# Moving the source dot products of a graph-attention layer one layer later, into the loop that uses them

## The chip, the cores and the metric

The kernel runs on one core of a Trainium2 chip. The metric is device time in microseconds (us), from the start of the program on the core to its end. One core has five engines that run side by side, each with an instruction queue of its own: PE (TensorE, matrix products), DVE (VectorE), ACT (ScalarE), POOL (GpSimd) and SP (SyncE, which here only issues transfers). Transfers are carried out by DMA engines; SP, ACT and POOL each issue some.

## The reference

Four graph-attention layers follow each other on 4096 nodes with 256 features. All use the same 0/1 matrix `adj` (4096 x 4096), and each ends in a layer norm of `x` plus the layer's result. Cut to what the change touches, with the layers counted from one:

```
x1 = layernorm(x  + additive attention with 4 heads(x, adj))
x2 = layernorm(x1 + scaled dot-product attention with 4 heads(x1, adj))
# third layer: additive attention with one head
h     = x2 @ W
e_src = h @ a[:256, 0]
e_dst = h @ a[256:, 0]
e     = leaky_relu(e_src[:, None] + e_dst[None, :], 0.01)
att   = softmax(where(adj > 0, e, -1e12), axis=1)
x3 = layernorm(x2 + elu(att @ h))
out = layernorm(x3 + cosine attention(x3, adj))
```

In the third layer each row i of the result needs one number of its own, `e_src[i]`, and one for each neighbour, `e_dst[j]`. The kernel takes exponentials of both apart. With the part that cancels in the softmax left out, the weight of a pair is max(exp(0.99 e_src[i]) exp(e_dst[j]), exp(0.01 e_dst[j])), which is computed as relu(row * dst - own) + own.

## The kernel before

The features stay in SBUF in one tile `X`, as 32 tiles of 128 nodes. Every layer goes through 8 blocks of 512 result rows, and within a block through all 4096 neighbours: in the first layer by tiles of 128, in the second by 64 tiles of 64 (index j), in the third by 16 pairs of tiles (index g), in the fourth by 32 tiles. The order of the work on PE, DVE and ACT in the second and third layers is the order in which the Python code writes it (`manual_schedule`); in the fourth layer's loop only the ending is written out so, and a scheduler orders the rest. Work that belongs to a finished block is spread by hand over the steps of the next block: the `finish(b, j)` and `finish(b, g)` functions say which step does what. Three steps (`LAG = 3`) lie between making a pair's weights and multiplying with them.

The second layer (`multi_head_attention`) makes scores on PE (L810), exponentials on ACT (L812), multiplies with the mask on DVE (L822), sums the weights into a tile `den` for the row sums, in part on POOL (L832) and in part by accumulating transfers that POOL issues (L838, `den<-prob`), and multiplies with V on PE (L846). The eight `prob` buffers of DVE come free when PE and these transfers have read them. The `finish` of a block turns, scales and normalises its 512 rows of x2. Four of its steps then make the dot products for the third layer, one tile at a time: `ga.dots(t)` multiplies the tile with two vectors in `a_row` (n = 0 for the source, n = 1 for the destination) and adds up along the row (L502, into `dot`). Then `ga.factors(b)` at j=57 takes the exponentials: for the source `src` (L510), which L515 stores to DRAM in the order of the nodes (`far<-src`, 128 partitions x 4 values, 512 elements of four bytes, on ACT's queue), and for the destination `dst`, `own` and `less`, which stay in SBUF.

The last block of the second layer has no next block, so its finishing is a generator, `tail` (L855 joins the parts of `den`, L868 makes the row sums on PE, L876 and L883 transpose, the layer norm follows, and at the end come the dots and factors of block 7). The third layer's block 0 takes three steps of it in each pair from g=2 on.

The third layer (`additive_one`) needs for block b the 512 values of `src` as one row, the same in all 128 partitions. `ga.row(b)` (L521) reads it back from DRAM on SP's queue; it waits there until the store has landed. Odd blocks keep it in the tile `a_row`, which the dots no longer need by then, and even ones in `first_row`. In each pair `weights(b, g)` issues the mask (L549, SP's queue, four buffers), makes relu(row * dst - own) on ACT (L556), adds `own` and multiplies with the mask on DVE (L557), and, in all blocks but the first, mixes the weights for a multiplication with fewer products (L434 on DVE, L435 and L436 on POOL). PE multiplies with X (block 0, L571) or with the mixed parts (L444, seven products per pair). After pair 15 ACT and DVE take the sums out of the accumulators (L450 to L458, `quarters`), and PE goes on to reuse an accumulator when it has been read. `finish` projects the sums with W on PE (L586), takes the elu and normalises; beside it the fourth layer's inputs are prepared (`follow`, with transfers `far<-squares` and `xT<-far` on SP's queue).

The fourth layer (`cosine_attention`) starts with its own scores (L1105); at tile (0, 1) it calls the third layer's `tail`, which makes the projection of its last block (L586).

Of the kernel before, what the change touches and what calls it, by code (L numbers as in the profile page):

```python
# [9 lines left out]
FP = mybir.dt.float32  # L10
# [3 lines left out]
AF = mybir.ActivationFunctionType  # L14
# [4 lines left out]
P = 128  # L19
D = 256  # L20
KC = D // P
QB = 4
QW = QB * P
# [5 lines left out]
def kernel(  # L29
# [27 lines left out]
    nc = tc.nc  # L57
    N = x.shape[0]
    NT = N // P
    NB = N // QW  # L60

    def pool(stack, name, bufs, **kw):
        return stack.enter_context(tc.tile_pool(name=name, bufs=bufs, reuse_waits="tile", **kw))
# [3 lines left out]
    fin = ctx.enter_context(tc.tile_pool(name="fin", bufs=2))  # L67
# [397 lines left out]
    class Additive:  # L465
# [30 lines left out]
                nc.vector.scalar_tensor_tensor(w[:, c, :D], pm[:, :D], -1.0 / D, w[:, c, :D], OP.mult, OP.add)  # L496
                nc.vector.memset(w[:, c, D:D + 1], 1.0 / D)

        def dots(self, t):
            for n in range(2):  # L500
                junk = fin1.tile([P, QW], FP, name="kept0")[:, :D]
                nc.vector.tensor_tensor_reduce(junk, X[:, t, :D], self.a_row[:, n, :], 1.0, 0.0, OP.mult, OP.add,  # L502
                                               self.dot[:, t, n:n + 1])

        def factors(self, b):

            t = slice(b * QB, (b + 1) * QB)
            s, d = self.dot[:, t, 0], self.dot[:, t, 1]
            src = fin.tile([P, QB], FP, name="src2")
            nc.scalar.activation(src, s, AF.Exp, scale=1.0 - self.slope)  # L510
            nc.scalar.activation(self.dst[:, t], d, AF.Exp)
            nc.scalar.activation(self.own[:, t], d, AF.Exp, scale=self.slope)
            nc.vector.tensor_scalar_mul(self.less[:, t], self.own[:, t], -1.0)
            far = self.rows[b] = self.far.tile([QB, P], FP, name=f"far2_{b}")
            nc.scalar.dma_start(far.rearrange("k p -> p k"), src)  # L515

        def row_of(self, b):
            return self.a_row.rearrange("p n f -> p (n f)") if b % 2 else self.first_row

        def row(self, b, eng):  # L520
            eng.dma_start(self.row_of(b), self.rows[b].rearrange("k p -> (k p)").unsqueeze(0).to_broadcast([P, QW]))  # L521
# [1 line left out]
    def additive_one(w_sb, ga, tail, op, follow):  # L523

        with ExitStack() as lay:
            mp = pool(lay, "gb_mask", 4)
            zp = pool(lay, "gb_z", 4)
            keep = pool(lay, "gb_mixed", 1)
# [15 lines left out]
            def weights(b, g):  # L544
                if b == 0 and g < 2:
                    mask = ga.first_mask[:, 2 * g:2 * g + 2, :]
                else:
                    mask = mp.tile([P, 2, QW], I32, name="mask")
                    nc.sync.dma_start(mask, edges[:, 2 * g:2 * g + 2, b * QW:(b + 1) * QW])  # L549
                if g == 13 and b < NB - 1:  # L550
                    ga.row(b + 1, nc.sync)
                z = prob[b, g] = zp.tile([P, 2, QW], FP, name="prob")
                for n in range(2):
                    j = 2 * g + n
                    r = pr.tile([P, QW], FP, name="r")
                    nc.scalar.activation(r, ga.row_of(b), AF.Relu, bias=ga.less[:, j:j + 1], scale=ga.dst[:, j:j + 1])  # L556
                    nc.vector.scalar_tensor_tensor(z[:, n, :], r, ga.own[:, j:j + 1], mask[:, n, :], OP.add, OP.mult)  # L557
                if b:
                    s = mix[b, g] = zp.tile([P, 4, HW], FP, name="mix")
                    mix_weights(s, z, nc.gpsimd)  # L560
# [74 lines left out]
            LAG = 3  # L635
# [3 lines left out]
            with tc.manual_schedule(engines=fixed):  # L639
                for i in range(len(units) + LAG):  # L640
                    b, g = units[i - LAG] if i >= LAG else (-1, 0)
                    if g == NP - 1:
                        sums(b, g)
                    if i < len(units):
                        weights(*units[i])
                    if b >= 0:
                        if g < NP - 1:
                            sums(b, g)
                        if b:
                            finish(b - 1, g)  # L650
                        else:
                            for _ in range(3 if g > 1 else 0):
                                next(before, None)
                            if g == 9:
                                follow.start()
                            elif g == 12:
                                follow.centre(bank())
                            if g % 2:
                                t = mixed[g // 2] = keep.tile([P, 2, 4, P], FP, name=f"mixed{g // 2}")
                                mix_features(t, g // 2)  # L660
                        if b > 1 and g in (2, 4, 6, 8, 9, 10, 11, 12, 13, 14, 15):
                            follow.prepare(bank, b - 2, 1, ys[b - 2])
                        if b == NB - 1 and g > 3 and g % 2 == 0:
                            q = g // 2 - 2
                            nc.scalar.dma_start(X[:, q * QB:(q + 1) * QB, :D], far_y[q])
                        if b == NB - 1 and g in (3, 5, 7):
                            follow.load_mask(0, (g - 3) // 2, prob[b, g][:, 0, :1])
# [11 lines left out]
    def multi_head_attention(w_sb, b_sb, tail, rows_of_den, rows_done, narrow_edges, ga):  # L679
# [12 lines left out]
        with ExitStack() as lay:  # L692
# [215 lines left out]
            def finish(b, j):  # L908

                rows = [X[:, b * QB + k, :D] for k in range(QB)]  # L910
                if j in (7, 9):
                    join_sums(b, j // 2 - 2)
                elif j == 12:
                    row_sums(halves(), b)
                elif j == 15:
                    bank = halves()
                    pd = turned_row_sums(bank, b)
                    po = turned_half(bank, b, 0)
                    reciprocals(pd, b)
                    half(po, b, 0)  # L920
                elif j == 18:
                    half(turned_half(halves(), b, 2), b, 2)
                elif j in (21, 23, 25, 27):
                    k = (j - 21) // 2
                    if k == 0:
                        mvs[b] = fin.tile([P, QB, 2], FP, name="mv")
                    one_row(mvs[b], k, rows[k])
                elif j == 29:
                    roots[b] = begin_root(mvs[b])
                elif j == 31:  # L930

                    end_root(*roots[b], nc.gpsimd)
                    lift_mean(mvs[b], *roots[b][:2], nc.gpsimd)
                elif j in (35, 37, 39, 41):
                    k = (j - 35) // 2
                    scale_row(rows[k], mvs[b], roots[b][1], k)
                if j + LAG - 1 in relief:

                    nc.vector.tensor_tensor(*late.pop(), OP.add)
                    ga.dots(b * QB + relief.index(j + LAG - 1))  # L940
                elif j == 57:
                    ga.factors(b)
                elif j == 63 and b == 1:
                    ga.row(0, nc.sync)
                elif j == 33 and b == NB - 2:
                    nc.gpsimd.dma_start(ga.first_mask, adjT.rearrange("(t p) i -> p t i", p=P)[:, :QB, :QW])
# [21 lines left out]
        def tail(bank):  # L968

            b = NB - 1  # L970
            for n in (1, 2):
                join_sums(b, n)
                yield
            yield
            row_sums(bank, b)
            yield
            yield
            reciprocals(turned_row_sums(bank, b), b)
            yield
            for k in (0, 2):  # L980
                half(turned_half(bank, b, k), b, k)
                yield
            mv = fin.tile([P, QB, 2], FP, name="mv")
            for k in range(QB):
                one_row(mv, k, X[:, b * QB + k, :D])
                yield
            v, r, n = begin_root(mv)
            yield
            end_root(v, r, n, nc.gpsimd)
            lift_mean(mv, v, r, nc.gpsimd)  # L990
            yield
            for k in range(QB):
                scale_row(X[:, b * QB + k, :D], mv, r, k)
                ga.dots(b * QB + k)
                yield
            ga.factors(b)
            rows_done()
            yield
# [78 lines left out]
    def cosine_attention(co, tail):  # L1077
# [4 lines left out]
        with ExitStack() as lay:  # L1082
# [137 lines left out]
            for i in range(len(units) + LAG):  # L1220
                if i < len(units):
                    b, j = units[i]
                    scores(b, j)
                    if j % 2:
                        weights(b, j // 2)
                    if (b, j) == (0, 1):
                        tail(bank, cp)
                    if (b, j) in steps:
                        n, step = steps[b, j]
                        co.prepare(bank, n, step, X[:, n * QB:(n + 1) * QB, :])  # L1230
# [104 lines left out]
```

## Time and profile before

| what | time |
|---|---|
| median of three runs | 2845.0 us (2840.16 to 2847.42) |
| profiled execution | 2831.88 us, of which 2830.1 us is the span of the profile |
| PE busy | 2784.8 us, 98% of the span |
| DVE / ACT / POOL busy | 2276.0 / 1694.8 / 1048.9 us |
| first layer | 0 to about 735 us |
| second layer, its loop over blocks | about 815 to 1728 us |
| third layer, block 0 | about 1728 to 1794 us |
| third layer, blocks 1 to 7 | about 1794 to 2190 us |
| fourth layer | about 2190 to 2830 us |

The profile comes from one execution. Busy time is the time in which an engine was carrying out an instruction. "A <- B: total, times, longest" in the list of waits means that engine and instruction group A was idle, and that B was what it last waited for. L numbers are lines of the kernel before; in the changed kernel the lines of the third layer stand 8 to 10 lower down.

### The profile page before, as it was taken

How to read it: one execution, taken by the hardware profiler on the slowest of the kernel's cores; microseconds unless marked ns; L12 is line 12 of the kernel's file. 1: busy time of each engine (PE TensorE's matmuls, PEld its weight loads, DVE VectorE, ACT ScalarE, POOL GpSimd, SP SyncE). 2: the span in 40 equal slices, each digit the busy share in tenths (PEclk: the TensorE clock that was granted, in tenths of full speed). 3: DMA queues.
4: the chain of work that ended last, by engine and by line, in shares of the span. 5: the costliest groups of instructions: out<-in, count | busy, mean ns of one | idle time of the engine just before them, and what ended most of it. 6: DMA issues, size and time to landing. Idle time of an engine off the chain costs nothing. (4 is left out here: it accounts for less than half of the span.)

```text
span 2830.1 us, 50179 instructions
## 1 busy us (share of the span) xinstructions
PE 2784.8 (98%) x19505; PEld 1433.5 (51%) x19505; DVE 2276.0 (80%) x3034; ACT 1694.8 (60%) x2641; POOL 1048.9 (37%) x983
## 2 busy tenths in 40 slices
PE   9999999999999999999999998999999999999998
PEld 4333333333543333333333333788888777777776
DVE  8899999999667778887887787888777766666665
ACT  8899999999246656666665655465555422222222
POOL 0001001010049878779778783345445000000000
PEclk9999999999999999999999999999999999999999
DMA  7566767665349898989999897566657544344341
GB/s 211 105 137 141 141 136 143 132 137 103 92 99 193 181 187 180 185 177 194 190 185 180 181 185 176 156 203 210 191 184 230 111 61 66 60 63 64 60 57 33
DMA packets 243650, 404.59 MB, mean 143 GB/s; under 512 B 25185, under 2 KB 126033, under 8 KB 242514
## 3 DMA queue, kind: packets, MB, share of 16 engines
q0 software_dynamic: 104176, 182.74, 40.8%
q1 hardware_dynamic: 132720, 211.41, 24.1%
q10 hardware_dynamic: 6514, 7.23, 0.7%
q8 instruction: 153, 2.51, 0.3%
q14 instruction: 87, 0.71, 0.1%
HBM read 332.27 MB, written 35.73 MB: 130 GB/s over the span
## 5 line engine op out<-in xcount | busy, mean ns | idle before, releaser
L822 DVE TENSOR_TENSOR prob<-p,mask 128x1024 f32<-128x1024 f32 x512 | 616.4, 1221 | 173.8 <-ACT p L812 136.9
L812 ACT ACTIVATE p<-p,shift 128x1024 f32<-128x1024 f32 x512 | 555.7, 1088 | 332.2 <-PE p L810 331.6
L310 PE MATMUL acc<-prob,V 128*32 128x512 f32 x6144 | 664.0, 592 | 1.2 <-DVE prob L300 1.2
L297 ACT ACTIVATE prob<-row,dst 128x512 f32<-128x512 f32 x1020 | 635.0, 712 | 0.6
L300 DVE SCALAR_TENSOR_TENSOR prob<-prob,mask 128x2048 f32<-128x2048 f32 x256 | 580.3, 2285 | 25.8 <-ACT prob L297 25.2
L832 POOL TENSOR_TENSOR den<-den,prob 128x1024 f32<-128x1024 f32 x220 | 557.4, 2534 | 81.7 <-DVE prob L822 73.7
L810 PE MATMUL p<-qT,kT 64*64 64x512 f32 x4096 | 533.2, 592 | 12.3 <-DVE prob L822 12.3
L846 PE MATMUL acc<-prob,V 64*64 64x512 f32 x4096 | 531.4, 590 | 0.0
L310 PEld LDWEIGHTS acc<-prob,V 128*32 128x32 f32 x6144 | 197.3, 110 | 453.0 <-issue 431.3
L444 PE MATMUL acc<-mix,mixed 128*128 128x256 f32 x1440 | 389.4, 380 | 1.4 <-DVE quarters L458 1.2
L810 PEld LDWEIGHTS p<-qT,kT 64*64 64x64 f32 x4096 | 154.0, 133 | 293.0 <-issue 232.8
L846 PEld LDWEIGHTS acc<-prob,V 64*64 64x64 f32 x4096 | 158.6, 133 | 282.0 <-issue 279.4
L444 PEld LDWEIGHTS acc<-mix,mixed 128*128 128x128 f32 x1440 | 271.9, 190 | 41.7 <-PE acc L444 3.5
L1117 DVE TENSOR_TENSOR prob<-prob,mask 128x1024 f32<-128x1024 f32 x128 | 156.5, 1223 | 167.1 <-ACT prob L1109 167.0
L90 POOL COPY tick<-prob 128x1 f32<-128x1 f32 x35 | 38.5, 1100 | 641.7 <-DVE prob L300 640.8
L838 POOL DMA_DIRECT2D den<-prob x240 | 223.2, 930 | 94.5 <-DMA den<-prob 41.4
L444 PE MATMUL acc<-prob,X 128*128 128x256 f32 x960 | 249.9, 380 | 6.4 <-DVE quarters L450 6.4
L1036 POOL DMA_DIRECT2D mask<-in_adjT x64 | 47.8, 747 | 518.8 <-DVE prob L1117 432.4
L557 DVE SCALAR_TENSOR_TENSOR prob<-r,own,mask 128x512 f32<-128x512 f32 x252 | 177.1, 744 | 72.3 <-POOL mix L436 24.2
L444 PEld LDWEIGHTS acc<-prob,X 128*128 128x128 f32 x960 | 181.1, 190 | 89.7 <-issue 61.7
L1109 ACT ACTIVATE prob<-p 128x512 f32<-128x512 f32 x144 | 86.2, 598 | 220.6 <-PE p L1105 208.6
L1109 ACT ACTIVATE prob<-g 128x512 f32<-128x512 f32 x112 | 66.8, 596 | 194.0 <-PE g L1105 194.0
(219 smaller groups left out, 2808.7 us busy)
## 6 DMA issues: line engine op xcount, KB each, us to landing
mask<-in_adjT SPq DMA_DIRECT2D x254, 512.0 KB
den<-prob POOLq DMA_DIRECT2D x240, 512.0 KB, 5.4
mask<-edges SPq DMA_DIRECT2D x512, 64.0 KB
mask<-in_adjT POOLq DMA_DIRECT2D x64, 512.0 KB, 5.6
edges<-in_adj POOLq DMA_DIRECT2D x32, 512.0 KB, 9.7
far<-squares SPq DMA_DIRECT2D x16, 512.0 KB
den<-prob SPq DMA_DIRECT2D x16, 512.0 KB
row<-far SPq DMA_DIRECT2D x7, 1024.0 KB
```

Source lines behind the costliest of these rows:

```text
L297: nc.scalar.activation(z[:, h, :], r, AF.Relu, bias=-1.0, scale=dst[:, j, h:h + 1])
L300: nc.vector.scalar_tensor_tensor(z, z, 1.0, mask[m][:, j % MJ, :].unsqueeze(1).to_broadcast([P, H, QW]), OP.add, OP.mult)
L310: nc.tensor.matmul(acc[b][h * G:(h + 1) * G, n, :], part, prob[b, j][:, h, :], start=(j == 0), stop=(j == NT - 1))
L444: nc.tensor.matmul(acc[at][:, half * HW:(half + 1) * HW], w, a, start=(g == 0 and half == 0), stop=(g == NP - 1), skip_group_check=True)
L557: nc.vector.scalar_tensor_tensor(z[:, n, :], r, ga.own[:, j:j + 1], mask[:, n, :], OP.add, OP.mult)
L810: nc.tensor.matmul(p[c * d:(c + 1) * d, r, :], kT[half, c, at:at + d], qT[half, c, cols], start=True, stop=True)
L812: nc.scalar.activation(p, p, AF.Exp, bias=shift)
L822: nc.vector.tensor_tensor(z, p, mask[m][:, j % MJ, :].unsqueeze(1).to_broadcast([P, KC, QW]), OP.mult)
L832: nc.gpsimd.tensor_tensor(to, to, flat, OP.add)
L838: nc.gpsimd.dma_start(to, flat, accum_op=OP.add)
L846: nc.tensor.matmul(acc[b][c][r * d:(r + 1) * d, :], V[half, j, r * d:(r + 1) * d], prob[b, j][half, r, :], start=(j == 0), stop=(j == NH - 1))
L1117: nc.vector.tensor_tensor(z, z, co.mask[b, 2 * g // MJ][:, lo:lo + 2, :], OP.mult)
```

## The change

Three things are moved.

First, `dots` takes a list of which dot products to make, and the tile for the unused elementwise product. In the second layer, `finish` makes both for block 0 and only the destination's for blocks 1 to 6, and the `tail` of block 7 makes only the destination's. The source's dot products for block b+1 are made in the third layer's block b, one tile in each of the pairs g=4 to 7. `factors` is cut in two: `sources(b)` has the exponential and the store of `src`. It runs in the second layer for block 0 (at j=59 instead of 57), and for block b+1 in the third layer's block b at g=8. The row is read back at g=11 instead of g=13. Since `a_row` is now in use in the third layer, odd blocks keep their row in a new tile `other_row`.

Second, the third layer's block 0 takes the steps of the second layer's `tail` from g=4 on instead of g=2, and the fourth layer's `start` and `centre` move from g=9 and 12 to g=11 and 14.

Third, the fourth layer calls the third layer's `tail`, with its last projection, at tile (0, 3) instead of (0, 1).

```diff
-        def dots(self, t):
-            for n in range(2):
-                junk = fin1.tile([P, QW], FP, name="kept0")[:, :D]
+        def dots(self, t, which, sb=fin1, name="kept0"):
+            for n in which:
+                junk = sb.tile([P, QW if sb is fin1 else D], FP, name=name)[:, :D]
                 nc.vector.tensor_tensor_reduce(junk, X[:, t, :D], self.a_row[:, n, :], 1.0, 0.0, OP.mult, OP.add,
                                                self.dot[:, t, n:n + 1])
...
+        def sources(self, b):
+            src = fin.tile([P, QB], FP, name="src2")
+            nc.scalar.activation(src, self.dot[:, b * QB:(b + 1) * QB, 0], AF.Exp, scale=1.0 - self.slope)
             far = self.rows[b] = self.far.tile([QB, P], FP, name=f"far2_{b}")
             nc.scalar.dma_start(far.rearrange("k p -> p k"), src)
...
-                if g == 13 and b < NB - 1:
-                    ga.row(b + 1, nc.sync)
+                if b < NB - 1:
+                    if 4 <= g < 4 + QB:
+                        ga.dots((b + 1) * QB + g - 4, (0,), sb, "h")
+                    elif g == 8:
+                        ga.sources(b + 1)
+                    elif g == 11:
+                        ga.row(b + 1, nc.sync)
...
-                            for _ in range(3 if g > 1 else 0):
+                            for _ in range(3 if g > 3 else 0):
                                 next(before, None)
-                            if g == 9:
+                            if g == 11:
                                 follow.start()
-                            elif g == 12:
+                            elif g == 14:
                                 follow.centre(bank())
...
-                    ga.dots(b * QB + relief.index(j + LAG - 1))
+                    ga.dots(b * QB + relief.index(j + LAG - 1), (1,) if b else (0, 1))
                 elif j == 57:
                     ga.factors(b)
+                elif j == 59 and b == 0:
+                    ga.sources(b)
...
-                ga.dots(b * QB + k)
+                ga.dots(b * QB + k, (1,))
...
-                    if (b, j) == (0, 1):
+                    if (b, j) == (0, 3):
                         tail(bank, cp)
```

More of the change, by code (lines that the diff above doesn't have):

```diff
@@ L507, in factors @@
             t = slice(b * QB, (b + 1) * QB)
-            s, d = self.dot[:, t, 0], self.dot[:, t, 1]
-            src = fin.tile([P, QB], FP, name="src2")
-            nc.scalar.activation(src, s, AF.Exp, scale=1.0 - self.slope)
+            d = self.dot[:, t, 1]
             nc.scalar.activation(self.dst[:, t], d, AF.Exp)
@@ L517, in row_of @@
         def row_of(self, b):
-            return self.a_row.rearrange("p n f -> p (n f)") if b % 2 else self.first_row
+            return self.other_row if b % 2 else self.first_row
         def row(self, b, eng):
@@ L525, in additive_one @@
         with ExitStack() as lay:
+            ga.other_row = pool(lay, "gb_row", 1).tile([P, QW], FP, name="other_row")
             mp = pool(lay, "gb_mask", 4)
```

## The prediction

> **What bounds the kernel now.** I read the page's engine table first, then the waits of TensorE stage by stage, then what the engine named there was itself waiting for, and last the DMA throughput in those places.
>
> ```profile
> span 2830.1 us, 50179 instructions
> ...
> PE 2784.8 (98%) x19505; PEld 1433.5 (51%) x19505; DVE 2276.0 (80%) x3034; ACT 1694.8 (60%) x2641; POOL 1048.9 (37%) x983
> ```
>
> PE is the bound. The change neither adds nor removes a matmul, so all that it can win is PE's idle time, some 36 us without the last wait at the end, and it can lose by adding to it. TensorE's waits in the second layer's loop (815 to 1728 us), and then in the third layer up to the fourth's start (1728 to 2200 us); total, times, longest:
>
> ```profile
> PE p L810 <- DVE prob L822: 12.3, 12, 2.2
> ```
>
> ```profile
> PE acc L444 <- DVE quarters L450: 6.4, 6, 1.5
> PE g L868 <- DVE den L855: 5.1, 1, 5.1
> PE g L586 <- DVE quarters L453: 2.7, 1, 2.7
> PE acc L571 <- DVE prob L557: 1.6, 1, 1.6
> PE acc L444 <- DVE quarters L458: 1.2, 6, 0.2
> ```
>
> Each group is touched by one part of the change. VectorE's waits in the second layer's loop say what stands behind the first:
>
> ```profile
> DVE prob L822 <- ACT p L812: 136.9, 253, 2.1
> DVE prob L822 <- DMA den<-prob: 29.5, 13, 4.1
> ```
>
> The first row is VectorE keeping pace. The second is not: in the timeline all thirteen lie 14 to 24 us after one of the eight issues of L515, the store `far<-src` that scatters 512 four-byte elements to DRAM. They hold up L822, and PE's gaps lie there: 1.26 and 2.02 us at 1043 and 1052 (issue 1028.5), 1.17 at 1169 (1146.8), 0.94 at 1283 (1260.8), 0.47 and 0.27 at 1396 and 1408 (1374.5), 0.40 and 1.88 at 1502 and 1511 (1488.5), 0.39, 0.46 and 2.20 at 1619 to 1627 (1603.8). Block 1, before the first such store, has none. Busy time by stretch (the last two columns are the DMA share and GB/s), the second and fourth rows beginning with such a store:
>
> ```profile
> 1020.00:1028.00 8.00, 8.00 (x80) 2.83 (x76) 7.66 (x11) 5.05 (x5) 4.35 (x4) 1.00 0.94 189
> 1028.00:1038.00 10.00, 10.00 (x100) 3.59 (x96) 7.95 (x8) 6.55 (x10) 8.40 (x5) 1.00 0.45 72
> ...
> 1720.00:1731.00 11.00, 9.41 (x77) 3.24 (x67) 8.50 (x11) 7.41 (x12) 8.11 (x6) 1.00 0.93 105
> ...
> 1773.00:1784.00 11.00, 11.00 (x29) 5.28 (x28) 9.80 (x21) 6.15 (x10) 0.00 (x0) 1.00 0.42 57
> ```
>
> For some 8 to 12 us after the store everything on the DMA engines crawls: 189 GB/s falls to 72. In detail the drop begins 2 to 3 us after the issue, and SP's L521, which waits for the store to land, issues 9 us after it. So the small store, not the dots, is what hurts the second layer, and I follow where the change puts it.
>
> [...] a store issued by ACT delays POOL's `den<-prob` (median 5.4 us to land, up to 14.3 after the store) and SP's masks. [...] the 9 us of 512 elements are this trace's number. [...]
>
> ```profile
> L502 DVE CUSTOM_DVE_ANT_0 kept<-X,a_row x64: 412/424/427, 1004.9 to 1772.5; 128x256 f32<-128x256 f32 x64
> L502 DVE DVE_READ_ACCUMULATOR2_ANT dot<- x64: 77/82/84, 1005.3 to 1772.8; 128x1 f32 x64
> ```
>
> [...] In the third layer `mix` L434 is 0.69 us and in places 0.87 to 1.72 with POOL's L435/L436 beside it, so a dot can come out longer than its row.
>
> **The change part by part**, on the profiled execution (2831.88 us).
>
> 1. *Second layer.* Stores for blocks 1 to 5 go from `finish`; block 0's stays (two tiles later, j=59). PE gaps after block 0's store are 1.26+2.02 = 3.28 of the 12.3; 0.8 at the loop's start is not a store's. Freed: 12.3 − 3.3 − 0.8 = **−8.2 us**. Block 6's store was at 1720 (next item). The 24 source dots and reads of finish for blocks 1 to 6 (each 0.42 + 0.08, about 0.45 as they overlap) leave VectorE, some 11 us, but VectorE waits for ACT here 137 us, so this is worth nothing on PE. Ends: −7 to −9; with the store's other place ±1.5.
>
> 2. *Transition and block 0 of the third layer* (1728 to 1794). VectorE's waits from 1724 to 1794:
>
> ```profile
> DVE prob L557 <- DMA mask<-in_adjT: 9.8, 4, 4.6
> ```
>
> Four waits for masks: 2.09 at 1733, 0.60 at 1735, 4.64 at 1741 (the crawl after 1720.05) and 2.48 at 1786 (after 1772.98). Both stores go. Without the first, L855's two additions (1745.5) no longer come last: VectorE is at most held by PE and is level with it by prob 7, and with the row sums asked for two pairs later (g>3), L868 should follow L855 without its 5.07 us, nor L571 with its 1.59, except that some of the 1.6 is the start of the layer. What is late next: `mixed` and the tail's rows share VectorE in pairs 6 to 15 with `centre` at g=14 and `factors`, each step 0.35 to 0.5 us, three steps per pair; four dots of block 1 (4×0.35) lie in pairs 4 to 7, where VectorE waits for PE. I take 5.0 of 5.07+1.59+0.50 = 7.2: **−5 us**; ends −7 and −1 (if VectorE stays the late one, two pairs cost it 5.7 us and PE 6.9, and about 4.9 of the gap stays).
>
> 3. *Third layer, blocks 1 to 6, the dots.* PE's work here is about 55.6 us per block, the period 57.2 to 57.5: VectorE with ACT and POOL sets the pace, as the end of each block shows (block 3, VectorE and PE):
>
> ```profile
> 1959.83 0.69 DVE L434 TENSOR_TENSOR mix<-prob 128x512 f32<-128x512 f32 x1
> 1960.44 0.68 DVE L450 TENSOR_TENSOR quarters<-one,acc 128x512 f32<-128x512 f32 x1
> ```
>
> ```profile
> 1961.17 0.70 PE L444 MATMUL acc<-prob,X 128*128 128x256 f32 x2 [1.45 <-DVE quarters L450]
> ```
>
> VectorE reaches L450 with no idle before it, PE waits 1.45. A dot thus lengthens the block unless VectorE is idle where it stands. Starts of 256-element operations in a row are 0.35 us apart (1743.12, 1743.47, 1743.80). At g=4, 5 and 7 VectorE runs without a pause; before g=6 it has 0.43 idle. Three exposed dots: 1.05 per block, 6 blocks: **+6.3 us** (block 7 makes none). The exponential (about 0.2) and the issue (0.37) on ACT at g=8 come where ACT waits for VectorE. Ends: 0 if the pauses of 1.64 at g=9 and 11 take them up, +10 if contention makes them 0.55.
>
> 4. *Third layer, the stores and the row.* Seven of them now fall in blocks 0 to 6, after pair 8. With block 4 as the pattern: the store goes out at about 1980, the crawl ends at about 1992. SP's queue then holds mask 11, the row (it waits for the store's landing, about 1989), masks 12, 13, 14. Behind the row, mask 12 goes out 5 us later than its 1984; mask 11 goes out with the store. They are wanted at 1995 (11), 1999, 2001 and 2006, so 1 to 4 us remain, a mask taking about 3.4 us normally; the fourth layer's `xT` loads (out at 1977.4 to 1979.2) land mostly before the crawl. The row itself is wanted at the next block's start, 18 us later. The half-used DMA queues (65% here, 90% in the second layer) are the cover. I take **0**; ends −0 and +3 us per block, since no store stands at this place before. A gain has no source here.
>
> 5. *Last projection at (0,3).* In the instruction order of the changed kernel, as before, the first two k (four L586) stand before the first scores; only the later two move. So the 2.7 us wait for L453 stays: VectorE is itself held up there 2.77 us by the load of `far<-squares` ahead of L453. **0**, ends ±1.
>
> Sum: −8.2 −5 +6.3 +0 +0 = **−6.9 us**, 2825.0 for the profiled execution. The median of runs lies 13.1 us above that execution, so 2845.0 − 6.9 = **2838**.
>
> **Rivals.** (B) *The third layer absorbs the dots* in ACT's and POOL's pauses (7.1 to 17.7 us in each kind of wait there, for); against: L450 is reached without a pause. Then −13.2: **2832**. (C) *The stores' crawl moves with them*, to where every block depends on masks: mask 11 or 12 late in each of blocks 1 to 6. For: block 0's mask waited 2.48 us after its store. Against: the 1 to 4 us left. At 3 us for six blocks it is +18 − 6.9 = +11: **2856**, slower than before; it decides from about 1.2 us per block on (6.9/6), and reaches 0.3% at 2.6. (D) *The transition does not gain*: VectorE stays late and the gap of 5 us only moves with g. Then −8.2 −1 +6.3 = −2.9: **2842**.
>
> **Chances and range.** As worked out 0.42, B 0.23, C 0.25, D 0.10. The 0.3% (8.5 us) is about what a measurement of this kernel can tell from no change. Around −6.9 the own range is −11 to −3 (2834 to 2842), of which a quarter passes −8.5: faster 0.23 + 0.12 = 0.35; same 0.30 + 0.08 of D + a little of C = 0.38; slower 0.27 with the tail of the ends of items 3 and 4. Eight in ten: from somewhat below B, 2828, to the middle of C, 2855.
>
> **What the profile after should show.** Item 1: PE's wait for L822 about 4 us, VectorE's for `den<-prob` only near 1043 to 1053. Item 2: no wait of PE at L868 and of VectorE for masks at 1733 to 1741; block 0 shorter by 5 us. Item 3: PE's wait at L444 for L450 (six of them) up from 6.4 to about 12.7. Item 4: no mask waits of VectorE in blocks 1 to 6; if they stand there with 2 to 4 us each, C is right. Item 5: the wait of L586 still about 2.7. Wrong altogether if the second layer's gaps remain without the stores.

## The result and the profile after

The changed kernel's median is 2819.11 us (2817.22 to 2819.99, six runs), beside 2841.4 us (2839.89 to 2847.42) for the kernel before: a ratio of 0.9917, 95% interval 0.9904 to 0.993. It is faster than before, and it lies 9 us below the range that was given (2828 to 2855). In a second session, with runs of both kernels beside the experiments, the changed kernel had 2818.29 us, the same, but the kernel before had 2833.24 us, a ratio of 0.9954 (0.9934 to 0.9973). The gain is thus 15 to 22 us, depending on the session, and nearly all of the difference between sessions is in the kernel before.

The profiled execution after has a span of 2816.0 us, 14.1 less than the 2830.1 of before. Busy times of the engines, from its page:

```profile
span 2816.0 us, 50179 instructions
...
PE 2784.7 (99%) x19505; PEld 1434.6 (51%) x19505; DVE 2274.4 (81%) x3034; ACT 1695.6 (60%) x2641; POOL 1050.6 (37%) x983
```

PE's busy time is the same to 0.1 us. The waits of PE in the second layer's loop, first, and from the third layer to the fourth's start, second, of the changed kernel (total, times, longest):

```profile
PE acc L579 <- DVE prob L565: 1.6, 1, 1.6
PE p L818 <- DVE prob L830: 0.8, 1, 0.8
```

```profile
PE acc L444 <- DVE quarters L450: 8.6, 6, 1.8
PE g L594 <- DVE quarters L453: 2.5, 1, 2.5
PE acc L444 <- DVE quarters L458: 1.0, 5, 0.2
```

The wait of the scores for `prob` fell from 12.3 to 0.8, the row sums' wait for `den` (5.1 before) is not there, and the six waits for L450 rose from 6.4 to 8.6. VectorE's wait for the accumulating transfers in the second layer fell from 29.5 to 0.5 us:

```profile
DVE prob L830 <- ACT p L820: 162.1, 314, 1.5
...
DVE prob L830 <- DMA den<-prob: 0.5, 1, 0.5
```

Waits alone do not add up to the span. The start of the first matmul of each stage (for the last row, the end of the span) gives the stages' lengths in us; the last column is an experiment (the changed kernel with the source dots put back into the second layer):

| stage | before | after | after less before | dots back |
|---|---|---|---|---|
| up to the second layer's first scores | 812.1 | 812.6 | +0.5 | 814.0 |
| second layer's loop | 916.9 | 900.7 | −16.2 | 901.9 |
| third layer, block 0 | 65.0 | 58.8 | −6.2 | 58.6 |
| third layer, blocks 1 to 7 | 400.4 | 406.6 | +6.2 | 399.9 |
| fourth layer | 635.7 | 637.3 | +1.6 | 637.6 |
| span | 2830.1 | 2816.0 | −14.1 | 2812.0 |

The gain is in the second layer and in block 0; the other blocks of the third layer give 6 us back. A second profile of each kernel (two of the experiments) has 915.7 and 901.4 us in the second layer's loop, 65.7 and 58.6 in block 0, 400.4 and 407.0 in blocks 1 to 7, and 637.9 and 637.1 in the fourth layer. So the second layer, block 0 and the other blocks repeat, within 2 us, and the +1.6 of the fourth layer does not.

The crawl of the DMA engines has not gone. In the changed kernel's stretches before and after a store of `src` in the third layer (issued at 1901.7; the last column is GB/s):

```profile
1894.00:1902.00 8.00, 8.00 (x39) 7.03 (x38) 7.83 (x18) 4.60 (x9) 3.63 (x5) 1.00 0.85 279
1904.00:1914.00 10.00, 10.00 (x48) 8.80 (x47) 8.12 (x16) 3.70 (x6) 4.25 (x6) 1.00 0.54 56
```

279 GB/s fall to 56 for ten us, as before; but PE (the figure after the comma) is busy for all of these ten us.

**What the second layer's stall really cost.** Its recorded idle fell by 11.5 us, its length by 16.2. The kernel before shows the rest in the two stretches behind block 0's store, here from its windows (the third column from the end is the granted clock of TensorE) and its PE timeline:

```profile
1055.00:1058.50 3.50, 3.50 (x23) 1.04 (x19) 3.36 (x4) 1.09 (x1) 3.36 (x4) 0.53 1.00 211
1058.50:1070.00 11.50, 11.50 (x120) 3.94 (x116) 8.24 (x8) 7.34 (x9) 10.42 (x7) 1.00 0.83 165
```

```profile
1054.21 1.09 PE L810 MATMUL p<-qT,kT 64*64 64x512 f32 x8 [2.02 <-DVE prob L822]
1055.12 1.88 PE L846 MATMUL acc<-prob,V 64*64 64x512 f32 x8
1056.76 1.95 PE L810 MATMUL p<-qT,kT 64*64 64x512 f32 x8
1058.46 1.11 PE L846 MATMUL acc<-prob,V 64*64 64x512 f32 x8
```

After a gap of 2.02 us the clock was at half for about 3.4 us (0.53 is the mean of the 3.5 us of the stretch), and the two rows of eight matmuls at 1055.12 and 1056.76 took 3.34 us up to the next row's start, in place of the usual 1.72: 1.6 us lost with PE "busy". Besides, in an undisturbed stretch four matmuls start every 0.43 us, as one group, but each is recorded as 0.589 long, so about 0.16 us of each gap is not counted as idle, and the first group after it is 0.05 us longer: about 0.2 us for each of twelve gaps, 2.5 in all. 11.5 + 1.6 + 2.3 (eleven gaps gone) is 15.4 of the 16.2; the remaining 0.8 is not explained. What halves the clock no run shows. The half clock came here behind a gap of 2.02 us, ten us after one of 1.26, but the length of a gap does not decide it in this trace. The longest gap of the same loop, 2.20 us, kept the full clock (1.00 from 1627 to 1632), and its matmuls took 1.09 us as usual:

```profile
1629.13 1.09 PE L810 MATMUL p<-qT,kT 64*64 64x512 f32 x8 [2.20 <-DVE prob L822]
```

So in this trace half the clock is a risk of a gap and not a fixed part of its price. The busy time of the whole kernel hides this loss, because the changed kernel has stretches at half clock of its own: 3.4 us at 2060, and 6.8 us at 2176, behind its wait of 2.5 us for L453. The second one covers the fourth layer's +1.6: its first eight scores take 5.5 us there, against 3.5 in the kernel before, whose wait of 2.7 us at this place left the clock full.

### The profile page after: what moved, and what is told of

It is laid out like the page before. It is cut to its first block, busy times and chain, and to the rows that moved or that the text cites. A ratio compares the mean times of both kernels' runs of the same rounds, so it can differ in the third digit from the quotient of the medians.

```text
span 2816.0 us, 50179 instructions
## 1 busy us (share of the span) xinstructions
PE 2784.7 (99%) x19505; PEld 1434.6 (51%) x19505; DVE 2274.4 (81%) x3034; ACT 1695.6 (60%) x2641; POOL 1050.6 (37%) x983
## 5 line engine op out<-in xcount | busy, mean ns | idle before, releaser
(220 smaller groups left out, 2810.3 us busy)
```

## The experiments

All ratios are to runs of the kernel before made beside the experiment.

**The kernel before again.** No edit.

> The kernel before, unchanged, to see whether its other executions stand 8 to 13 us above the one that was profiled because the same gaps grow. Theory 1 (the store's crawl takes a different length from execution to execution): if this profiled execution is near 2840, its TensorE gaps behind L822 in the second layer sum to about 20 us in place of 12.3, and no other group of waits grows by more than 1 us. Rival 2 (the difference is no wait of TensorE, but the chip's or the clock's): gaps as before, with busy time or clock changed.

2834.05 us (2825.37 to 2840.61, 12 runs; ratio 1.0004, 0.9991 to 1.0017). Its profiled execution, 2836.64 us, has 11.4 us of waits for `prob`, like the one shown before, and 5.5 at L868. So theory 1 fails as it was put: the gaps did not grow to 20 us. Its granted clock was 0.995, not 0.998, and PE's busy time 2792.1 us, not 2784.8, so rival 2 holds for this execution. The two belong together. Leaving out the last ten us, the clock stood at half for 20.5 us here (behind the waits at 1058, 1748, 2079 and 2195), and for 6.8 us in the profile shown before (at 1055 and 1748): waits of nearly the same length, but more time at half clock behind them. At half speed 13.7 us more are 6.8 us of work, about the growth of the busy time. (The span grew by only 4.8 us, 3.1 of them ahead of the second layer, so this is not the whole account.) What stays is the spread: 15 us over 12 runs here, against 3.6 us over five runs of the changed kernel below.

**The store two tiles later, nothing else.** `factors` is cut in two as in the change, and `sources` runs for every block in the second layer.

```diff
             elif j == 57:
                 ga.factors(b)
+            elif j == 59:
+                ga.sources(b)
...
         ga.factors(b)
+        ga.sources(b)
         rows_done()
```

> The kernel before, with nothing moved but the exponential and store of the source factors: two tiles later (j=59 in place of 57) in every block of the second layer; in the tail it stays behind the factors. All 64 dots stay where they were. Theory 1 (the place of the store among the accumulating transfers decides): block 0's gaps of 3.3 us went in the changed kernel although its store stayed, so here all of the second layer's gaps go: 12.3 to about 1 us, 11 us less in the profile; the 5 us at L868 stays. Rival (a store anywhere in the second layer costs about 1.6 us of TensorE): gaps remain at 8 to 12 us and the time is that of before within 3 us. Rival (the dots' leaving is what helped): the same, no gain.

2826.07 us, 0.997 (0.9961 to 0.998), 7 us faster. TensorE's waits of this kernel from the second layer to the row sums:

```profile
PE g L870 <- DVE den L857: 7.2, 1, 7.2
PE p L812 <- DVE prob L824: 4.5, 6, 1.6
```

Two tiles take away two thirds of the second layer's idle time, so the place of the store counts (its stage is 905.3 us long, 11.6 less); the gap at the row sums grew to 7.2 us, with 10.2 us at half clock from 1735 on, and took part of it back: block 0 of the third layer is 68.6 us long, 3.6 more. The crawl itself is milder at the new place (the table further below); why, no run shows.

**The changed kernel with the source dots back in the second layer.**

```diff
-                    if 4 <= g < 4 + QB:
-                        ga.dots((b + 1) * QB + g - 4, (0,), sb, "h")
-                    elif g == 8:
+                    if g == 8:
...
-                    ga.dots(b * QB + relief.index(j + LAG - 1), (1,) if b else (0, 1))
+                    ga.dots(b * QB + relief.index(j + LAG - 1), (0, 1))
...
-                ga.dots(b * QB + k, (1,))
+                ga.dots(b * QB + k, (0, 1))
```

> The changed kernel with the 28 source dots put back into the second layer; only the exponentials, stores and rows are made in the third layer. Theory 1 (stores): second layer's gaps stay below 1.5 us and L868's stay away; the third layer's waits for L450 fall from 8.6 back to about 6.4, so this is 2 to 3 us faster than the changed kernel. Rival (dots were the load in the second layer): its gaps come back to some 8 us or more, slower than the changed kernel by 6.

2811.44 us (2810.3 to 2813.76), 0.992 (0.9904 to 0.9937). Its waits in blocks 1 to 7 of the third layer:

```profile
PE acc L444 <- DVE quarters L450: 4.9, 6, 1.4
PE g L592 <- DVE quarters L453: 2.1, 1, 2.1
```

The second layer stays nearly free of gaps (1.6 us) with all dots in it: the dots were no load there. In the third layer they are: this kernel is 7 us faster than the changed one, and its blocks 1 to 7 are 6.7 us shorter. The change would have been better without the part that names it. Once more, later:

> The changed kernel with the source dots put back into the second layer, once more, beside the turned store: 2811 us, third layer 400 us. If it is level with the turned store within 2 us, moving the store and mending it are worth the same, and the dots' move costs the changed kernel 6 to 7 us.

2811.24 us, 0.9918 (0.9902 to 0.9935).

**The kernel before with block 0's store alone.** In `factors`, before the store: `if b: self.rows[b] = self.rows[0]; return`. The kernel leaves out the stores of blocks 1 to 7 and reads block 0's row for them.

> The kernel before without the stores of blocks 1 to 7: their rows are read from block 0's factors (so the third layer's weights are wrong from block 1 on, the amount of work is not). All dots stay in the second layer, and block 0's store stays at j=57. Theory 1 (stores): gaps in the second layer 12.3 to about 4 (block 0's 3.3 and 0.8), L868's 5 us gone, mask waits of VectorE at the third layer's start gone: 13 us less in the profile, and at least as much in the runs. Rival (dots): no change within 3 us.

2820.05 us, 0.9952 (0.9934 to 0.997), 13 us faster with nothing moved. Block 0's gap stood here with 3.8 us, with 6.8 us at half clock around its end; all others of the second layer were gone, but for the 0.8 at its start, and L868's was 2.3. The stores are the cause, together with what waits for their landing.

**The parts alone.** The changed kernel again, and each part by itself on the kernel before (the edits are those of the change).

> The changed kernel, unchanged, beside its three parts on one chip. Theory (the stores): ratio to before 0.992 again, and a spread between executions of some 3 us against 14 us of the kernel before, because the crawls that vary in length no longer hold TensorE. Rival (the 22 us of the first comparison were partly the chip): the runs differ by the 14 us by which the two profiles differ, ratio 0.995.

2818.29 us (2815.95 to 2819.57), 0.9954. Here the difference of the medians, 15 us, is about that of the profiles, 14.1.

> Only the first part of the change (dots, stores and rows); tail steps from g=2, start and centre at g=9 and 12, last projection at (0, 1). Theory (the stores): nearly all of the gain, the ratio 0.993, second layer's gaps under 1.5 us, and at the row sums L868 some 2 us left, as where only the stores were dropped (2.27 us there). Rival (the later tail did the 5 us at L868): the 5 us stand there again and the gain falls to about 15 us.

2823.61 us, 0.9966 (0.9956 to 0.9975): 10 of the 15 us. L868 kept a wait of 2.2 us, as expected.

> The kernel before with only the second part: tail steps from g=4, start and centre at g=11 and 14. Theory (late masks hold VectorE at the start of the third layer, so two pairs later it is still the late one): the gap at L868 stays at 4 to 5 us, the time is that of before within 2 us. Rival (the row sums were just asked for too early): the gap goes, 4 to 5 us faster.

2833.8 us, 1.0001 (0.999 to 1.0012). Its gap at L868 was 2.8 us, so the gap shrank, while the second layer's gaps were 14.6 us in this execution and nothing was gained. It pays only with part 1.

> The kernel before with only the third part, the last projection at (0, 3). The prediction's step: no difference within 1 us, the wait of 2.7 us for L453 stays. Rival: the wait goes, 2 to 3 us faster.

2832.56 us, 0.9999 (0.9988 to 1.001); the wait for L453 stood with 3.2 us.

**The changed kernel without the third layer's stores.** The same lines as for one store, in `sources`.

> The changed kernel without the stores of blocks 1 to 7 (their rows are read from block 0's factors, so the third layer's weights are wrong from block 1 on; the amount of work is not). Theory (the third layer covers the stores): same time as the changed kernel within 1.5 us (2818), ratio to before about 0.995, and the third layer's length of 406 us as there. Rival (its 6 us more than before come from the stores, not the dots): the third layer falls to about 400 us and the whole is 6 us faster.

2821.02 us, 0.9947 (0.9933 to 0.9962): no faster than the changed kernel. Its blocks 1 to 7 take 406.7 us, against 406.6 there. The third layer, with its crawls at 56 GB/s, pays nothing for them; the 6 us there belong to the dots, which this kernel has.

**What makes the DMA engines crawl.** Four kernels made from the one before, alike but for the store. In the last two, block 0's store stays as it is, and blocks 1 to 7 read block 0's row; in the first, the row's values come in another order. The amount of work is the same.

```diff
 # one 16-byte element per partition
-            nc.scalar.dma_start(far.rearrange("k p -> p k"), src)
+            nc.scalar.dma_start(far.rearrange("k p -> (k p)").rearrange("(p k) -> p k", k=QB), src)
 # twice
+            again = self.far.tile([QB, P], FP, name=f"again_{b}")
+            nc.scalar.dma_start(again.rearrange("k p -> p k"), src)
 # 64 bytes apart (blocks 1 to 7)
+                far = self.far.tile([QB, P, 16], FP, name=f"far2_{b}")[:, :, 0]
 # 8 bytes apart, by partition (blocks 1 to 7)
+                far = self.far.tile([P, QB, 2], FP, name=f"far2_{b}")[:, :, 0].rearrange("p k -> k p")
```

> The kernel before with each store as 128 elements of 16 bytes in place of 512 of four (so the row's order is wrong from the start of the third layer, the amount of work is not). Theory (the crawl is paid per element): crawls of 2 to 3 us in place of 8 to 12, the second layer's gaps fall from 12 to 2 us or less, L868's 5 us goes or halves: 15 us faster. Rival (any store to DRAM at this place stops the queues for its landing): gaps and time as before.

> The kernel before with each store issued twice, the second to another place in DRAM. Theory (the crawl is paid per element): each crawl doubles to some 20 us, more than the eight weight buffers and their transfers can bridge, so each of seven costs TensorE 5 us or more: 30 to 60 us slower. Rival (the crawl is a fixed event, such as the landing): under 5 us slower.

> The kernel before, with the stores of blocks 1 to 7 as 512 elements of four bytes that lie 64 bytes apart in DRAM (32 KB in place of 2 KB); the rows of these blocks are read from block 0's factors, so the third layer's weights are wrong from block 1 on, the amount of work is not. Theory A (neighbouring four-byte places written from different partitions disturb each other): crawls go in blocks 1 to 7, and the time is that of the kernel with one store, 0.995 of before. Theory B (four-byte elements as such): crawls and gaps stay, time within 3 us of before.

> The kernel before, with the stores of blocks 1 to 7 as 512 elements of four bytes, eight bytes apart, the four of a partition next to each other (4 KB); rows of these blocks read from block 0's factors, as in the run with 64 bytes, so the third layer's weights are wrong from block 1 on. Theory A (neighbours from different partitions disturb each other): few neighbours are of another partition, so the crawls shrink to 3 us or less, about 0.995 of before. Theory B (four-byte elements as such): crawls of 8 us and more and gaps of 8 to 12 us in the second layer as before, ratio 0.998 to 1.

| store | time, us | ratio | wait for `prob`, us | GB/s behind the stores |
|---|---|---|---|---|
| as in the kernel before | | | 12.3 | 58 to 92 |
| as before, two tiles later | 2826.07 | 0.997 (0.9961 to 0.998) | 4.5 | 96 to 165 |
| twice 512 x 4 bytes | 2833.32 | 0.9991 (0.9981 to 1.0) | 9.4 | 51 to 95 |
| 512 x 4, 8 bytes apart | 2816.94 | 0.9944 (0.9926 to 0.9961) | 4.1 | 120 to 150 |
| 128 x 16 bytes | 2814.21 | 0.9923 (0.9906 to 0.9939) | 0.8 | 171 to 192 |
| 512 x 4, 64 bytes apart | 2819.44 | 0.9949 (0.9933 to 0.9964) | 3.2 | 188 to 193 |

The wait is TensorE's in the second layer. The last column is the rate of all DMA engines from 1 to 11 us after the issue, over the stores of this form in the second layer's loop (six, or five where block 0's is left as it was). Block 1's store in five kernels, in the order of the table without its second row; the last figure is GB/s:

```profile
1147.80:1157.80 10.00, 10.00 (x99) 3.65 (x95) 7.25 (x8) 6.59 (x8) 6.89 (x5) 1.00 0.61 86
```

```profile
1143.70:1153.70 10.00, 10.00 (x96) 3.46 (x92) 7.28 (x8) 6.27 (x7) 6.89 (x5) 1.00 0.98 95
```

```profile
1146.00:1156.00 10.00, 10.00 (x100) 3.71 (x96) 7.19 (x8) 6.85 (x8) 7.10 (x6) 1.00 0.76 120
```

```profile
1142.90:1152.90 10.00, 10.00 (x96) 3.64 (x92) 7.27 (x8) 6.59 (x8) 8.80 (x7) 1.00 0.91 181
```

```profile
1147.80:1157.80 10.00, 10.00 (x100) 3.70 (x96) 7.21 (x8) 6.59 (x8) 8.73 (x7) 1.00 1.00 193
```

Theory "per element" falls with the doubled store: 1024 elements, in two places, cost no more than 512. The same 512 four-byte elements are harmless where they lie 64 bytes apart, so their size and number alone are not the cause. It is the places: in the kernel's layout sixteen separate writes, from sixteen partitions, fall into each 64 bytes of DRAM (64 is only the unit that I count by); with 8 bytes between them eight do, and the crawl is milder; with 16-byte elements four do, and it is short (54 GB/s from 1143.9 to 1145.9, then the full rate); with 64 bytes apart one, and there is none. Two things change together across these kernels, how many writes share 64 bytes and how often neighbours come from different partitions, so these runs do not tell the two apart. Nor is the time lost in the store's own packets: in the kernel before the 528 packets of the queue that carries block 0's store all fall into 1030 to 1033, where they take 10.7% of the 16 engines' time, and the crawl outlasts them (49 GB/s from 1033 to 1039). With 64 bytes apart block 1's store has as many packets, which take 8.8% of the engines' time from 1148 to 1151.5, and no crawl follows. Where in the memory or the DMA engines the time goes, no run shows.

The times of the last two kernels do not rank their stores, because block 0's gap is in both and makes up most of their waits, once without and once with half the clock behind it. First 8 bytes apart, whose next half clock comes at 2176, then 64 bytes apart, where the longer record (1.70 us) shows it:

```profile
1054.05 1.09 PE L814 MATMUL p<-qT,kT 64*64 64x512 f32 x8 [3.32 <-DVE prob L826]
```

```profile
1054.17 1.70 PE L814 MATMUL p<-qT,kT 64*64 64x512 f32 x8 [2.15 <-DVE prob L826]
```

After a gap of 3.32 us the clock thus stayed full, and after one of 2.15 it did not.

**Block 0's store back at j=57 in the changed kernel.**

```diff
                 elif j == 57:
+                    if b == 0:
+                        ga.sources(b)
                     ga.factors(b)
-                elif j == 59 and b == 0:
-                    ga.sources(b)
```

> The changed kernel with block 0's store back at j=57 in the second layer. Theory (two tiles decide whether accumulating transfers are caught in the crawl): block 0's gaps of 3 to 4 us come back near 1043 to 1055 us, with TensorE at half its clock behind them: 4 to 6 us slower than the changed kernel, 2823. Rival (block 0's gaps went for another reason): 2818 as there.

2825.09 us, 0.9964 (0.9951 to 0.9977): 7 us above the changed kernel's median in another session, and 4 us above the kernel of the same session that has the changed one's second layer (2821.02). Its second layer's loop is 908.4 us long, 7.7 more than the changed kernel's. TensorE's waits there:

```profile
PE p L818 <- DVE prob L830: 5.1, 2, 4.3
```

One store, moved by two tiles, costs 4.3 us of gap and, as in the kernel before, half the clock behind it (6.8 us of it here, 3.4 there).

**The store mended where it stands.** The kernel before with part 2, and with the store turned on VectorE first, so that it goes out in runs of 128 bytes, in the right order.

```diff
...
+            turned = fin.tile([P, P // QB], FP, name="src2_turned")
+            nc.vector.transpose(turned, self.src)
+            n = P // QB
+            for q in range(QB):
+                nc.scalar.dma_start(far[:, q * n:(q + 1) * n], turned[q * n:q * n + QB, :])
-            nc.scalar.dma_start(far.rearrange("k p -> p k"), src)
...
```

> The kernel before with the second part of the change alone, and with each store turned first on VectorE (one 32x32 block transpose of 128x32) and sent as four transfers of four runs of 128 bytes, in the right order; nothing is moved out of the second layer. Both theories: no crawls, the second layer's gaps under 1.5 us, the third layer as long as before (400 us): 2811 to 2814 us, 20 us faster than before and some 5 us faster than the changed kernel. Rival (four issues in a row on ACT, 1.5 us, hold up the exponentials there): TensorE gaps of about 1 us per block at L810, 2820.

2821.41 us, 0.9952 (0.9936 to 0.9969), as the rival said. ACT's timeline of this kernel at the first store:

```profile
1031.59 1.33 ACTq L520 DMA_DIRECT2D far<-src_turned  x4
1032.97 3.10 ACT L817 ACTIVATE p<-p,shift 128x1024 f32<-128x1024 f32 x3 [2.87 <-DMA far<-src_turned]
```

The exponentials wait 2.87 us behind the issues, half of it for the transpose. With `nc.sync` in place of `nc.scalar`:

> The kernel with the turned store, its four transfers issued by SP in place of ACT. Theory (ACT's queue was held, not the DMA engines): the TensorE gaps of 0.7 to 1.2 us per block behind L810 go, 5 us or more less in the second layer, 2811 to 2814 us in all, 0.992 to 0.993 of before. Rival (the four small transfers delay others): gaps stay, 2820; or SP's masks, queued behind the wait for the transpose, come late and gaps move to them.

2813.2 us, 0.9909 (0.9888 to 0.993). TensorE's waits in the second layer, first with ACT issuing, then with SP:

```profile
PE p L815 <- DVE prob L827: 5.5, 7, 1.2
```

```profile
PE p L815 <- DVE prob L827: 0.8, 1, 0.8
```

All runs of this kernel and of the changed kernel with the dots back (2811 us) lie below all runs of both kernels of the change, and the intervals of the two overlap.

## Why the prediction was wrong

The cause was named rightly: the stores, not the dots, held up the second layer. The direction of every term was right too. The number of the store's elements was not what made it dear: the store with 64 bytes between them has 512 as well, and no crawl (188 to 193 GB/s behind it). The step that failed is item 1, where a store's cost was taken to be the idle time recorded for TensorE, and block 0's share of it was taken to stay. Of the 7.2 us between the sum, −6.9, and the profiles, −14.1, item 1 is 8.0, item 2 1.2 and item 3 0.1; what lies ahead of the second layer and the fourth layer took 2.1 back. The time failed a second time where the sum was put on the median of the runs.

- *Item 1, the second layer* (−8.2, ends −7 to −9): measured −16.2 (−14.3 in the second pair of profiles). Two terms were mis-sized. "Block 0's stays" kept 3.3 us of gaps, and the ±1.5 for the store's other place did not cover them; two tiles later they were gone, and put back they cost 4 to 8 us in all. And a gap was priced at its recorded idle time, while half the clock behind one of them and the uncounted end of each added 4.7 us, of which 3.9 are accounted for above.
- *Item 2, transition and block 0* (−5): measured −6.2. The wait at L868 went, the 1.6 us at L571 stayed, as the working allowed. This gap, too, had more behind it than its 5.07 us: the clock stood at half from 1748.1 to 1751.5. No wait for a mask comes where those of 1733 to 1741 were; one of 3.4 us stands earlier, near the start of the layer, and is covered. Part 2 was needed for the last 2 us of it.
- *Item 3, the dots* (+6.3): measured +6.2, and +6.7 against the kernel with the dots back. The sum is right, the distribution is not: one exposed cost in each of six blocks was forecast, and only four have one. By their first matmuls, blocks 1 and 2 are as long as with the dots back (52.7 and 56.3 us), and blocks 3 to 6 have 58.3, 58.3, 58.1 and 59.2 against 57.1, 57.0, 56.7 and 56.9. That four dearer blocks come to the same sum is luck. Block 6 holds a stretch at half clock after its gap of 1.77 us:

```profile
2059.50:2063.00 3.50, 3.50 (x10) 2.55 (x9) 3.43 (x7) 1.48 (x2) 0.92 (x2) 0.53 0.58 207
```

  The waits for L450 rose to 8.6, not 12.7: the blocks grew by more than these waits show.
- *Item 4, stores and row in the third layer* (0): held. They crawl as feared, and the run without them is no faster. Rival C, the slower side, had 0.25 of the chance and found nothing; one wait of VectorE for a mask, 2.0 us, stands in the whole third layer after block 0.
- *Item 5* (0): held, alone and in the whole.
- *Base.* "The median of runs lies 13.1 us above that execution" was carried over as a constant. The changed kernel's median stands 1.3 us above its own profiled execution. The kernel before varies by 15 us within a session and by 8 us between two sessions, the changed kernel by 4 us and 1 us. The granted clocks of these executions say what much of this is. Of the 90 runs of the kernel before made beside the experiments, the six with a mean clock of 0.998 took 2828.6 us on average, and the twenty with 0.995 took 2838.0. By an estimate from these figures 0.003 of the clock over 2830 us is 8.5 us, nearly all of that difference. So the slower executions are mainly those with more time at half clock, and the kernel with more gaps runs that risk more often: the kernels without a stall in the second layer are narrow (1 to 5 us over four to six runs, 6 over thirteen). It is not the whole, since runs with the same 0.997 reach from 2824.7 to 2837.0. Why the first session was 8 us slower stays open; its runs of the kernel before have no clock on record. The chip is one possible reason: in the experiments, made on four chips, that kernel's medians reach from 2833 to 2838 us.

The shape of the range was wrong for the same reason: it was bounded by the recorded idle time of one execution, and reached 17 us above the estimate, to 2855, towards a mechanism that came to nothing.

## What to carry to other kernels

A store of a column of four-byte elements, whose neighbours in DRAM come from different partitions, slowed the DMA engines here for some ten us (279 GB/s to 56 in the changed kernel). Such a store is worth turning first, so that it writes runs, and issuing from a queue that nothing urgent stands behind (a ratio of 0.9909 here from SP's queue, 0.9952 from ACT's, both with part 2), before any work is moved around it. A stall of TensorE can cost more than its recorded gap (1.6 us more behind the one of 2.02 us): look at the granted clock just behind it, and in more than one execution. And work that costs next to nothing on an engine with idle time in one stage can cost its full price in a stage where that engine sets the pace: the source dots made the second layer's loop 1.2 us longer, no more than two profiles of one kernel differ there (915.7 and 916.9), and the third layer's blocks 1 to 7 6.7 us.

## What was not expected of the hardware

1024 scattered four-byte writes took no longer to clear than 512 (51 to 95 against 58 to 92 GB/s during ten us), and behind the same 512 at 64 bytes' distance the rate stayed at 188 to 193 GB/s. The DMA engines stayed slow after the store's own packets had left them (49 GB/s from 1033 to 1039 in the kernel before, the packets all before 1033). Gaps of TensorE of 1.77 us (the changed kernel), 2.02 (the kernel before) and 2.15 (64 bytes apart) were followed by half of its clock, for 3.4 us after the first two, while gaps of 2.20 and 2.71 (the kernel before) and 3.32 us (8 bytes apart) were not.
